# Message passing on a graph: edge tiles of 128 in place of 125, and the node update's inputs prepared another way

## The chip, the cores and the metric

The kernel runs on one core of a Trainium2 chip. The metric is the device time of one execution in microseconds (us). Engines are called PE (matmul), PEld (its weight load), DVE (vector), ACT (scalar), POOL (GpSimd, which here issues the gathers) and SP (which issues plain DMAs).

## The reference

A layer norm with a relu gives h from x (12,500 nodes, 64 features). One graph layer follows over 412,500 edges that are sorted by receiver:

```python
h = maximum(layernorm(x), 0)
m_in = concat([h[src], h[dst], edge_attr], -1)           # 64 + 64 + 32
msg  = swish(m_in @ W1 + b1) @ W2 + b2                   # 64 units
att  = softmax(swish(m_in @ Wa1 + ba1) @ Wa2 + ba2, axis=0)   # over all edges
agg  = segment_sum(msg * att, dst)
out  = x + swish(concat([h, agg], -1) @ Wu1 + bu1) @ Wu2 + bu2
```

All is float32. A node has 33 incoming edges on average, so some 1000 consecutive edges have about 30 receivers.

## The kernel before

**Node stage.** x is normalized, h is transposed into `hT` (features on partitions, kept in SBUF and written once to `hT_d`), and the product of h with the senders' part of [Wa1, W1] goes to a table in HBM, `ts_d`, of 128 columns a node; the receivers' part goes to `tr_d`.

**The group loop** (`one_pass`) does nearly all of the work. A group is K = 8 tiles of EP = 125 edges; there are NG = 413. For group g + 2, `load` issues:

- on POOL one indirect DMA per tile (L513), which gathers the senders' rows of `ts_d` into `gs`, one row per partition. A tile with odd j gathers 126 rows (WIDE), one more than it has edges;
- on SP the window of receiver rows (L534, 40 rows from the group's first receiver on) and, every fourth group, edge features and receiver numbers (L524, L527);
- on DVE the one-hot matrix of receivers (L538), and on PE the product of one-hot matrix and edge features with the window (L542), which adds the receivers' and the edges' parts in one matmul.

**Chosen groups.** In one group of three (`chosen`) the eighth tile is not gathered. ACT copies one column of `hT` per edge into `cols` (L484), at an address that it loads into a register, and PE multiplies `cols` with `stack` (L548). `numbers` loads the senders' numbers on SP, `places` works out the columns on six small DVE instructions (L467 to L473), and `burst` spreads the copies over three groups by the table `SLOTS`, some 36 to 48 per group in two portions.

**The rest of a group.** `begin(g)` adds the gathered rows (L553, DVE) and takes tanh (L556, ACT). `end(g)` makes messages and logits (L566 to L577, DVE). Every four groups `top` and `weigh` update the softmax's running maximum (L596 on PE, L603 to L610). `sum_up`, some groups later, weighs a group (`by_node`, L620 on DVE and L626 on PE), copies the sum (L632, ACT), projects it (L637, PE) and adds it into `sums` (`put`, L651 to L658, DVE). The compute instructions of the loop are pinned in program order on each engine. `gs` has seven buffers, `pe` three; POOL waits when no `gs` is free.

**Inputs of the update.** While groups 17 and later run, one of 13 node tiles is prepared every eight groups: `tile_bias` (at g % 8 of 1 and 5) reads h back from `hT_d` into `hb` on SP (L329) behind a memset of a row of ones on DVE (L327), multiplies it with Wu1's upper half and bu1 (L331) and copies the result into `bu` on ACT (L348), which goes out to `bq_d` (L351). `tile_rest` (at 3) loads x rows into another `hb` (L366), adds bu2 on DVE (L370) and writes `xb_d` (L371). `hb` has two buffers for all of these. None of these three kinds of compute instruction is pinned.

**The end.** The last groups run in smaller batches, and the update of all nodes follows. A branch to a general version (`general`) is taken only where a group's receivers do not fit its window.

Of the kernel before, what the change touches and what calls it, by code (L numbers as in the profile page):

```python
# [44 lines left out]
F32 = mybir.dt.float32  # L45
I32 = mybir.dt.int32
AF = mybir.ActivationFunctionType
ALU = mybir.AluOpType
# [3 lines left out]
DRAM = bass.MemoryType.DRAM  # L52

P = 128
EP = 125
D = 64
DE = 32
U = 64
C = 2 * U
# [13 lines left out]

EVERY = 3
PHASE = 1
SLOTS = (((0, 24), (24, 24)), ((48, 24), (72, 12)), ((84, 24), (108, 17)))
ROUND = 12582912.0
WIDE = 126
EPS = 1e-5
NEG = -3.0e38  # L80
BIG = 3.0e38


PARTS = [("pair", 4 * C), ("we", C), ("bias", C), ("wu2h", 2 * D), ("wa2", U), ("bu2", D), ("w_bu", U),
         ("w2b", U), ("wu1a", U), ("wu2", D), ("ba2", 1)]
HALVED = 4
WHY = "a receiver's number; windows past the last node are padded"

# [2 lines left out]
def gnn_kernel(ctx: ExitStack, tc: tile.TileContext, n_edges, x, src, src_row, dst, dst_row, first, edge,  # L91
# [32 lines left out]
    wu2h = part["wu2h"].rearrange("p (h d) -> p h d", h=2)  # L124
    we, bias, wa2, bu2_r, ba2_c = (part[k] for k in ("we", "bias", "wa2", "bu2", "ba2"))
    w_bu = part["w_bu"][:D + 1]
    w2b = part["w2b"][:S1]
    wu1a, wu2 = part["wu1a"][:U], part["wu2"][:U]

# [191 lines left out]
def node_bias(tc, b, v, work, ps):  # L321

    nc = tc.nc
    NB, w_bu = v["NB"], v["w_bu"]
    n = min(4, NB - b)
    hb = work.tile([D + 1, 4, P], F32, name="hb")
    nc.vector.memset(hb[D:, :, :], 1.0)  # L327
    for r in range(2):
        nc.sync.dma_start(hb[:D, r:n:2, :], v["hT_d"][r * D:(r + 1) * D, b // 2:(b + n) // 2, :])  # L329
    pb = ps.tile([P, 4, P], F32, name="mt")  # L330
    nc.tensor.matmul(pb[:U, :n, :], w_bu, hb[:, :n, :], start=True, stop=True)  # L331
    return pb[:U, :n, :]


def tile_bias(tc, c, first, v, work, ps, bus):

    nc = tc.nc
    m = min(NC, v["NB"] - c)
    if first:
        bus[c] = work.tile([U, P * NC], F32, name="bu", bufs=1)[:, :P * m]  # L340
    elif m <= 4:
        return
    i = 0 if first else 4
    n = min(4, m - i)
    pb = node_bias(tc, c + i, v, work, ps).rearrange("u b (h p) -> u h p b", h=2)
    to = bus[c].rearrange("u (h k p b) -> u k h p b", h=2, k=2, b=m // 2)
    for k in range(i // (m // 2), (i + n) // (m // 2)):
        nc.scalar.copy(to[:, k], pb[:, :, :, k * m // 2 - i:(k + 1) * m // 2 - i])  # L348
    if i + n == m:
        for h in range(2):  # L350
            nc.sync.dma_start(v["bq_d"][c // NC, h * U:(h + 1) * U, :P // 2 * m],  # L351
                              bus[c][:, h * P // 2 * m:(h + 1) * P // 2 * m])


def halves(ap, c, n, k, NB):
# [1 line left out]
    return ap.rearrange("(h p b) d -> p h b d", h=2, b=NB)[:, :, c + k * n // 2:c + (k + 1) * n // 2, :]  # L357


def tile_rest(tc, c, v, work):  # L360

    nc = tc.nc
    n = min(NC, v["NB"] - c)
    xt = work.tile([P, 4, P], F32, name="hb").rearrange("p a b -> p (a b)")[:, :n * D]
    for k in range(2):
        nc.sync.dma_start(  # L366
            xt[k * P // 2:(k + 1) * P // 2].rearrange("p (h b d) -> p h b d", h=2, d=D),
            halves(v["x"], c, n, k, v["NB"]))
    xv = xt.rearrange("p (b d) -> p b d", d=D)
    nc.vector.tensor_tensor(xv, xv, v["bu2_r"][:, None, :].to_broadcast([P, n, D]), ALU.add)  # L370
    nc.sync.dma_start(v["xb_d"][c // NC, :, :n * D], xt)  # L371


def one_pass(tc, n_edges, v):
    nc = tc.nc
    NB, T, NG, NP, NT = (v[k] for k in ("NB", "T", "NG", "NP", "NT"))
    ident, iota_w, bj, dloc, src_full, base_sb, real, unreal, far, wrong = (
        v[k] for k in ("ident", "iota_w", "bj", "dloc", "src_full", "base_sb", "real", "unreal",
                       "far", "wrong"))
    ts_d, tr_d, bq_d, xb_d, edge, dst_row = (  # L380
        v[k] for k in ("ts_d", "tr_d", "bq_d", "xb_d", "edge", "dst_row"))
# [10 lines left out]
    with ExitStack() as ctx:  # L392
# [3 lines left out]
        NH = NP // 2  # L396
        sums = keep.tile([P, NH + 2 * W], F32, name="sums")
        stand = keep.tile([P, NH + 2 * W], F32, name="stand")
        base_lo = keep.tile([1, NG + 1], I32, name="base_lo")
        base_hi = keep.tile([1, NG + 1], I32, name="base_hi")  # L400
# [35 lines left out]
        with tc.tile_pool(name="work2", bufs=2) as work2, \  # L436
# [50 lines left out]
                for i in range(EVERY):  # L487
                    columns(g + 3 + i, *SLOTS[EVERY - 1 - i][k])

            at_sp, at_lo, at_hi, bus = {}, {}, {}, {}  # L490


            tr_w = bass.AP(tensor=tr_d.tensor, offset=tr_d.offset,
# [10 lines left out]
            def load(g):  # L504

                t = g * K
                if g % NQ == 0:
                    registers(g, ENG.SP, at_sp)
                full = gather.tile([P, K, C], F32, name="gs")
                gs = gss[g] = full[:EP]  # L510
                for j in range(K - (g in chosen)):
                    rows = WIDE if j % 2 == 1 else EP
                    nc.gpsimd.indirect_dma_start(  # L513
                        out=full[:rows, j, :], out_offset=None, in_=ts_d[:, :],
                        in_offset=bass.IndirectOffsetOnAxis(ap=src_full[:rows, t + j:t + j + 1], axis=0))
                if g % NQ == 0:
                    n = min(NQ, NG - g) * E2
                    eo = eos[g // NQ % 2]
# [199 lines left out]
            for g in range(NG):  # L718
# [17 lines left out]
                burst(g, 0)  # L736
                if g + AHEAD < NG:
                    load(g + AHEAD)
                numbers(g + EVERY + 4)
                places(g + EVERY + 3)  # L740
                if more:
                    next(more)
                if g == NG - 1:
# [20 lines left out]
                if g == min(44, NG):  # L764
# [5 lines left out]
                if g == min(45, NG):  # L770
                    pin(nc.vector.tensor_reduce(worst, worst_ps, AX.X, ALU.max))
                    pin(nc.vector.tensor_scalar(wrong, worst, 0.0, None, op0=ALU.is_gt))
                if g >= 16 and g // 8 - 2 < NT:
                    c = (g // 8 - 2) * NC
                    if g % 8 in (1, 5):
                        tile_bias(tc, c, g % 8 == 1, v, work2, one_ps, bus)
                    elif g % 8 == 3:
                        tile_rest(tc, c, v, work2)

            tc.mark_branch_hint_location("again", "LikelyTaken",  # L780
                                         engines=[ENG.SP, ENG.DVE, ENG.PE, ENG.Activation])
# [271 lines left out]
def _laid_out(w):  # L1053

    import numpy as np

    first = np.concatenate([w["Wa1"], w["W1"]], axis=1)
    part = {k: np.zeros((P, n), np.float32) for k, n in PARTS}
    for r in range(2):
        for h in range(2):  # L1060
            at = (2 * r + h) * C
            part["pair"][h * D:(h + 1) * D, at:at + C] = first[r * D:(r + 1) * D]
    for r in (0, 64, 96):
        part["we"][r:r + DE] = first[2 * D:]
# [6 lines left out]
    part["w_bu"][:D + 1] = np.concatenate([w["Wu1"][:D], w["bu1"][None]])  # L1071
    part["w2b"][:S1] = np.concatenate([w["W2"], w["b2"][None]])
# [43 lines left out]
```

## Time and profile before

| | |
|---|---|
| median of 23 runs | 5638.05 us (5618.55 to 5668.15) |
| the profiled execution | 5626.18 us, its span 5624.3 us |
| mean granted clock of TensorE | 0.594 |
| first tanh of the group loop, last one | 101 us, 5573 us after the span's start |
| DMA | 398.57 MB, mean 71 GB/s |

The page counts busy time per engine, without register, semaphore and DMA-issuing instructions. A row of a group of instructions reads: line, engine, operation, output<-input, count | busy us, mean ns of one | idle us of the engine ahead of them, and what ended most of it. "issue" there is idle time in which the engine waited for nothing that the profile shows; "remote" is a semaphore whose setter it could not name. A line of the timeline begins with its start and its length in us.

### The profile page before, as it was taken

The page shows a single profiled execution, that of the slowest core. Times are in us where ns is not written, and L with a number is a line of the kernel's source. Part 1 is how long each engine was busy: PE and PEld are TensorE (multiplying, and loading weights), DVE is VectorE, ACT ScalarE, POOL GpSimd, SP SyncE. Part 2 cuts the span into 40 slices and gives each one's busy share as a digit, 9 for nine tenths or more (in the row PEclk, how much of TensorE's full clock was granted, in tenths as well). Part 3 has the DMA queues.
Part 4 walks back from the last instruction along what each step waited for, and adds up shares of the span by engine and source line. Part 5 has one row for each costly group of instructions (what it writes and reads, how often), then busy time and mean ns, then how long its engine had stood idle before and what let it go on. Part 6 is the DMA issues. An engine that isn't in the chain of part 4 may idle for free. (4 is left out here: it accounts for less than half of the span.)

```text
span 5624.3 us, 81803 instructions
## 1 busy us (share of the span) xinstructions
PE 2571.5 (46%) x11509; PEld 2005.7 (36%) x11509; DVE 3352.7 (60%) x9768; ACT 2489.0 (44%) x17651; POOL 3544.7 (63%) x3198
## 2 busy tenths in 40 slices
PE   5244444444444444444444444444444444444445
PEld 4233333333333333333333333333333333333335
DVE  6366656666556555555555565565555555555657
ACT  3244444444444444444444444444444444444422
POOL 4666666666666666666666666666666666666663
PEclk8565566666656555555555565555555555565556
DMA  7233333233232222222222222222222222222232
GB/s 228 61 73 70 74 81 78 70 80 75 68 70 65 63 63 67 58 66 61 65 66 63 63 67 59 66 61 65 66 61 65 68 58 65 61 66 65 63 81 68
DMA packets 335625, 398.57 MB, mean 71 GB/s; under 512 B 170293, under 2 KB 266088, under 8 KB 334690
## 3 DMA queue, kind: packets, MB, share of 16 engines
q0 software_dynamic: 205168, 205.98, 15.6%
q1 hardware_dynamic: 128530, 177.64, 13.2%
q10 hardware_dynamic: 1376, 9.67, 0.4%
q14 instruction: 457, 3.74, 0.2%
q8 instruction: 94, 1.54, 0.1%
HBM read 365.34 MB, written 25.72 MB: 70 GB/s over the span
## 5 line engine op out<-in xcount | busy, mean ns | idle before, releaser
L513 POOL DMA_INDIRECT gs<-ts_d,src_sb x3173 | 3527.4, 1112 | 1988.7 <-issue 1893.2
L484 ACT COPY cols<-hT 128x1 f32 x16375 | 1903.7, 188 | 2528.0 <-issue 2472.1
L542 PE MATMUL pe<-wins,eo 128*125 128x256 f32 x3304 | 1507.3, 633 | 837.1 <-DVE lg L577 250.8
L542 PEld LDWEIGHTS pe<-wins,eo 128*125 128x125 f32 x3304 | 1000.7, 319 | 1172.3 <-DVE lg L577 289.0
L637 PE MATMUL mt<-ss,w2u 65*128 65x40 f32 x826 | 226.5, 371 | 1325.9 <-DVE gm L603 583.4
L620 DVE TENSOR_SCALAR wt<-iota_w,dloc,p 125x40 f32<-125x40 f32 x3304 | 751.1, 332 | 1.6
L637 PEld LDWEIGHTS mt<-ss,w2u 65*128 65x128 f32 x826 | 209.5, 296 | 1473.1 <-issue 861.3
L626 PE MATMUL sp<-wt,acts 125*65 125x40 f32 x6608 | 721.1, 287 | 11.8 <-issue 8.4
L626 PEld LDWEIGHTS sp<-wt,acts 125*65 125x65 f32 x6608 | 684.2, 205 | 18.3 <-issue 12.0
L566 DVE SCALAR_TENSOR_TENSOR acts<-pe,gs 125x512 f32<-125x512 f32 x413 | 284.4, 689 | 572.3 <-ACT pe L556 475.7
L553 DVE TENSOR_TENSOR gs<-pe,gs 125x1024 f32<-125x1024 f32 (+1 forms) x413 | 486.4, 1178 | 177.0 <-remote 123.2
L556 ACT ACTIVATE pe<-gs 125x1024 f32<-125x1024 f32 x413 | 422.6, 1023 | 337.8 <-DMA gs<-ts_d,src_sb 128.7
L655 DVE TENSOR_TENSOR sums<-sums,mt 64x40 f32 x606 | 115.6, 191 | 489.8 <-remote 456.2
L596 PE MATMUL mt<-ident,mx 125*128 125x125 f32 x110 | 47.9, 436 | 595.1 <-remote 242.0
L538 DVE TENSOR_SCALAR eo<-dbs,bj 64x250 f32<-64x250 int32 x826 | 290.0, 378 | 17.1 <-DMA dbs<-in_dst_row_dram 7.6
L574 DVE TENSOR_TENSOR pe<-pe,w_all 125x512 f32<-125x512 f32 x413 | 288.8, 699 | 13.4
L572 DVE SCALAR_TENSOR_TENSOR pe<-pe,gs 125x512 f32<-125x512 f32 x413 | 286.8, 695 | 9.2
L577 DVE TENSOR_REDUCE lg<-pe 125x8 f32<-125x512 f32 x413 | 283.8, 687 | 9.5
L547 DVE SCALAR_TENSOR_TENSOR cols<-num,half,cols 128x125 f32<-128x125 int32 x131 | 45.6, 348 | 372.1 <-ACT cols L484 320.2
L596 PEld LDWEIGHTS mt<-ident,mx 125*128 125x128 f32 x110 | 20.0, 181 | 606.7 <-remote 440.9
L691 DVE SCALAR_TENSOR_TENSOR total<-total,scale,psum 125x1 f32<-125x1 f32 x110 | 23.5, 214 | 294.0 <-ACT p L610 270.6
L548 PE MATMUL pe<-stack,cols 128*125 128x128 f32 x262 | 79.9, 400 | 203.5 <-DVE cols L547 125.5
(125 smaller groups left out, 1211.7 us busy)
## 6 DMA issues: line engine op xcount, KB each, us to landing
eo<-in_edge_dram SPq DMA_DIRECT2D x103, 500.0 KB
dbs<-in_dst_row_dram SPq DMA_DIRECT2D x206, 250.0 KB
gs<-ts_d,src_sb POOLq DMA_INDIRECT x3173
wins<-tr_d SPq DMA_DIRECT2D x826, 32.0 KB
num<-in_src_row_dram SPq DMA_DIRECT2D x131, 62.5 KB
ts_d<-ts SPq DMA_DIRECT2D x5, 896.0 KB
tr_d<-tr ACTq DMA_DIRECT2D x5, 896.0 KB
hT_d<-hT ACTq DMA_DIRECT2D x1, 3136.0 KB
```

The source lines that it names most:

```text
L484: pin(nc.scalar.copy(to[:, first + i:first + i + 1], hT[:, bass.ds(regs[i], 1)]))
L513: nc.gpsimd.indirect_dma_start(out=full[:rows, j, :], out_offset=None, in_=ts_d[:, :], in_offset=bass.IndirectOffsetOnAxis(ap=src_full[:ro ...
L538: pin(nc.vector.tensor_scalar(eo[:WR, e], db[:, e], bj[g // NQ % 2 * WR:(g // NQ % 2 + 1) * WR, g, h:h + 1], None, op0=ALU.is_equal))
L542: pin(nc.tensor.matmul(pe[:, 2 * q:2 * q + 2, :], eo[:, q * EP:(q + 1) * EP], win[:, q // 2, :, :], start=True, stop=q < H - 1 or g not in ...
L553: pin(nc.vector.tensor_tensor(gss[g][:, :n, :], pes[g][:, :n, :], gss[g][:, :n, :], ALU.add))
L556: pin(nc.scalar.activation(pes[g], gss[g], AF.Tanh))
L566: pin(nc.vector.scalar_tensor_tensor(acts[g % ACTS][:, :, 0:U], th[:, :, U:C], 1.0, gs[:, :, U:C], op0=ALU.add, op1=ALU.mult))
L572: pin(nc.vector.scalar_tensor_tensor(att, th[:, :, 0:U], 1.0, gs[:, :, 0:U], op0=ALU.add, op1=ALU.mult))
L574: pin(nc.vector.tensor_tensor(att, att, wa2[:EP, None, :].to_broadcast([EP, K, U]), ALU.mult))
L620: pin(nc.vector.tensor_scalar(wt[:, j, :], iota_w[:EP, j // H, :], dloc[:, g * K + j:g * K + j + 1], p[:, k + j:k + j + 1], op0=ALU.is_equ ...
L626: pin(nc.tensor.matmul(sp, acts[g % ACTS][:, j, :], wt[:, j, :], start=j == 0, stop=j == K - 1))
L637: pin(nc.tensor.matmul(pp, w2u.rearrange("s h u -> s (h u)"), sps.pop(g), start=True, stop=True))
```

## The change

EP becomes 128, so a group has 1024 edges, NG is 403 and a tile fills all partitions. Every gather takes EP = 128 rows, and WIDE goes. The last portion of columns grows from 17 to 20, so that a chosen tile has 128 of them.

`tile_bias` no longer reads `hT_d`: one matmul of a block-diagonal weight (`w_bup`, Wu1's upper half twice) with `hT` as it lies in SBUF gives four node blocks at once, and two DVE additions of `bu1` write them to `bu`. All of it is pinned and stands right behind `places` in the loop. The DMAs to `bq_d` are issued at g % 8 of 7 (`tile_bias_out`). `tile_rest` is split over three groups: x rows are asked for at 0 into a buffer of their own (`xt`), bu2 is added at 3, `xb_d` is written at 6. The numbers of `numbers` and `places` are written out with the same values. Two small tables of bases share a tile, and the check of the windows moves from groups 44 and 45 to 46 and 47.

```diff
-EP = 125
+EP = 128
-SLOTS = (((0, 24), (24, 24)), ((48, 24), (72, 12)), ((84, 24), (108, 17)))
+SLOTS = (((0, 24), (24, 24)), ((48, 24), (72, 12)), ((84, 24), (108, 20)))
-WIDE = 126
...
 def tile_bias(tc, c, first, v, work, ps, bus):
...
-    pb = node_bias(tc, c + i, v, work, ps).rearrange("u b (h p) -> u h p b", h=2)
+    pb = ps.tile([P, 4, P], F32, name="mt")[:, :n // 2, :]
+    pin(nc.tensor.matmul(pb, v["w_bup"], v["hT"][:, (c + i) // 2:(c + i + n) // 2, :], start=True, stop=True))
     to = bus[c].rearrange("u (h k p b) -> u k h p b", h=2, k=2, b=m // 2)
-    for k in range(i // (m // 2), (i + n) // (m // 2)):
-        nc.scalar.copy(to[:, k], pb[:, :, :, k * m // 2 - i:(k + 1) * m // 2 - i])
-    if i + n == m:
-        for h in range(2):
-            nc.sync.dma_start(v["bq_d"][c // NC, h * U:(h + 1) * U, :P // 2 * m],
-                              bus[c][:, h * P // 2 * m:(h + 1) * P // 2 * m])
+    for b in range(i, i + n):
+        r, k = b % 2, b // (m // 2)
+        if b >= i + 2 and m // 2 > 1:
+            continue
...
+        pin(nc.vector.tensor_scalar(
+            to[:, k, :, :, at:at + 2 * q - 1:2],
+            pb[rows, (b - i) // 2:(b - i) // 2 + q, :].rearrange("u q (h p) -> u h p q", h=2),
+            v["bu1"][rows], None, op0=ALU.add))
...
-def tile_rest(tc, c, v, work):
+def tile_rest(tc, c, step, v, work, rest):
...
+    if step == 0:
+        xt = rest[c] = work.tile([P, 4 * P], F32, name="xt", bufs=1)[:, :n * D]
+        for k in range(2):
+            nc.sync.dma_start(
+                xt[k * P // 2:(k + 1) * P // 2].rearrange("p (h b d) -> p h b d", h=2, d=D),
+                halves(v["x"], c, n, k, v["NB"]))
+    elif step == 1:
+        xv = rest[c].rearrange("p (b d) -> p b d", d=D)
+        tc.keep_in_program_order(
+            nc.vector.tensor_tensor(xv, xv, v["bu2_r"][:, None, :].to_broadcast([P, n, D]), ALU.add))
+    else:
+        nc.sync.dma_start(v["xb_d"][c // NC, :, :n * D], rest.pop(c))
...
-                full = gather.tile([P, K, C], F32, name="gs")
-                gs = gss[g] = full[:EP]
+                gs = gss[g] = gather.tile([P, K, C], F32, name="gs")[:EP]
                 for j in range(K - (g in chosen)):
-                    rows = WIDE if j % 2 == 1 else EP
                     nc.gpsimd.indirect_dma_start(
-                        out=full[:rows, j, :], out_offset=None, in_=ts_d[:, :],
-                        in_offset=bass.IndirectOffsetOnAxis(ap=src_full[:rows, t + j:t + j + 1], axis=0))
+                        out=gs[:, j, :], out_offset=None, in_=ts_d[:, :],
+                        in_offset=bass.IndirectOffsetOnAxis(ap=src_sb[:, t + j:t + j + 1], axis=0))
...
-                numbers(g + EVERY + 4)
-                places(g + EVERY + 3)
+                numbers(g + 7)
+                places(g + 6)
+                if g >= 16 and g // 8 - 2 < NT and g % 8 in (1, 5):
+                    tile_bias(tc, (g // 8 - 2) * NC, g % 8 == 1, v, work2, one_ps, bus)
                 if more:
                     next(more)
...
-                    if g % 8 in (1, 5):
-                        tile_bias(tc, c, g % 8 == 1, v, work2, one_ps, bus)
-                    elif g % 8 == 3:
-                        tile_rest(tc, c, v, work2)
+                    if g % 8 == 7:
+                        tile_bias_out(tc, c, v, bus)
+                    elif g % 8 in (0, 3, 6):
+                        tile_rest(tc, c, g % 8 // 3, v, work2, rest)
```

More of the change, by code (lines that the diff above doesn't have):

```diff
@@ L84 @@
 PARTS = [("pair", 4 * C), ("we", C), ("bias", C), ("wu2h", 2 * D), ("wa2", U), ("bu2", D), ("w_bu", U),
-         ("w2b", U), ("wu1a", U), ("wu2", D), ("ba2", 1)]
+         ("w2b", U), ("wu1a", U), ("wu2", D), ("ba2", 1), ("w_bup", 2 * U), ("bu1", 1)]
 HALVED = 4
@@ L126, in gnn_kernel @@
     w_bu = part["w_bu"][:D + 1]
+    w_bup, bu1 = part["w_bup"], part["bu1"]
     w2b = part["w2b"][:S1]
@@ L337, in tile_bias @@
     nc = tc.nc
+    pin = tc.keep_in_program_order
     m = min(NC, v["NB"] - c)
@@ L344, in tile_bias @@
     n = min(4, m - i)
-    pb = node_bias(tc, c + i, v, work, ps).rearrange("u b (h p) -> u h p b", h=2)
+    pb = ps.tile([P, 4, P], F32, name="mt")[:, :n // 2, :]
+    pin(nc.tensor.matmul(pb, v["w_bup"], v["hT"][:, (c + i) // 2:(c + i + n) // 2, :], start=True, stop=True))
     to = bus[c].rearrange("u (h k p b) -> u k h p b", h=2, k=2, b=m // 2)
-    for k in range(i // (m // 2), (i + n) // (m // 2)):
-        nc.scalar.copy(to[:, k], pb[:, :, :, k * m // 2 - i:(k + 1) * m // 2 - i])
-    if i + n == m:
-        for h in range(2):
-            nc.sync.dma_start(v["bq_d"][c // NC, h * U:(h + 1) * U, :P // 2 * m],
-                              bus[c][:, h * P // 2 * m:(h + 1) * P // 2 * m])
+    for b in range(i, i + n):
+        r, k = b % 2, b // (m // 2)
+        if b >= i + 2 and m // 2 > 1:
+            continue
+        q = 2 if m // 2 > 1 else 1
+        rows = slice(r * U, (r + 1) * U)
+        at = b - k * (m // 2)
+        pin(nc.vector.tensor_scalar(
+            to[:, k, :, :, at:at + 2 * q - 1:2],
+            pb[rows, (b - i) // 2:(b - i) // 2 + q, :].rearrange("u q (h p) -> u h p q", h=2),
+            v["bu1"][rows], None, op0=ALU.add))
@@ L355, in halves, with tile_bias_out @@
+def tile_bias_out(tc, c, v, bus):
+    m = min(NC, v["NB"] - c)
+    for h in range(2):
+        tc.nc.sync.dma_start(v["bq_d"][c // NC, h * U:(h + 1) * U, :P // 2 * m],
+                             bus[c][:, h * P // 2 * m:(h + 1) * P // 2 * m])
 def halves(ap, c, n, k, NB):
     return ap.rearrange("(h p b) d -> p h b d", h=2, b=NB)[:, :, c + k * n // 2:c + (k + 1) * n // 2, :]
-def tile_rest(tc, c, v, work):
+def tile_rest(tc, c, step, v, work, rest):
     nc = tc.nc
     n = min(NC, v["NB"] - c)
[L364 to L371, printed above, removed]
+    if step == 0:
[10 more added lines that the diff above has]
+        nc.sync.dma_start(v["xb_d"][c // NC, :, :n * D], rest.pop(c))
@@ L376, in one_pass @@
     NB, T, NG, NP, NT = (v[k] for k in ("NB", "T", "NG", "NP", "NT"))
-    ident, iota_w, bj, dloc, src_full, base_sb, real, unreal, far, wrong = (
-        v[k] for k in ("ident", "iota_w", "bj", "dloc", "src_full", "base_sb", "real", "unreal",
+    ident, iota_w, bj, dloc, src_sb, base_sb, real, unreal, far, wrong = (
+        v[k] for k in ("ident", "iota_w", "bj", "dloc", "src_sb", "base_sb", "real", "unreal",
                        "far", "wrong"))
@@ L398, in one_pass @@
         stand = keep.tile([P, NH + 2 * W], F32, name="stand")
-        base_lo = keep.tile([1, NG + 1], I32, name="base_lo")
-        base_hi = keep.tile([1, NG + 1], I32, name="base_hi")
+        bases = keep.tile([33, NG + 1], I32, name="bases")
+        base_lo, base_hi = bases[0:1], bases[32:33]
         nc.vector.memset(base_lo, 0)
@@ L488, in burst @@
                     columns(g + 3 + i, *SLOTS[EVERY - 1 - i][k])
-            at_sp, at_lo, at_hi, bus = {}, {}, {}, {}
+            at_sp, at_lo, at_hi, bus, rest = {}, {}, {}, {}, {}
             tr_w = bass.AP(tensor=tr_d.tensor, offset=tr_d.offset,
@@ L763, in one_pass @@
                     pin(nc.vector.tensor_reduce(far[:, 1:2], dloc, AX.X, ALU.min, negate=True))
-                if g == min(44, NG):
+                if g == min(46, NG):
                     worst = small.tile([EP, 1], F32, name="worst", bufs=1)
@@ L769, in one_pass @@
                     pin(nc.tensor.transpose(worst_ps, worst.to_broadcast([EP, EP]), ident[:EP, :EP]))
-                if g == min(45, NG):
+                if g == min(47, NG):
                     pin(nc.vector.tensor_reduce(worst, worst_ps, AX.X, ALU.max))
@@ L1071, in _laid_out @@
     part["w_bu"][:D + 1] = np.concatenate([w["Wu1"][:D], w["bu1"][None]])
+    for r in range(2):
+        part["w_bup"][r * D:(r + 1) * D, r * U:(r + 1) * U] = w["Wu1"][:D]
+    part["bu1"][:, 0] = np.tile(w["bu1"], 2)
     part["w2b"][:S1] = np.concatenate([w["W2"], w["b2"][None]])
```

## Prediction

> **What bounds the kernel now.** I read the page first: no engine is busy for more than 63% of the span, so no engine's plain work is the bound, and the question is what the engines wait for. The chain of work that ended last holds only the last memsets and says nothing. The groups of the page name two long streams of small instructions, and the answer lies in how they share time:
>
> ```profile
> span 5624.3 us, 81803 instructions
> PE 2571.5 (46%) x11509; PEld 2005.7 (36%) x11509; DVE 3352.7 (60%) x9768; ACT 2489.0 (44%) x17651; POOL 3544.7 (63%) x3198
> L513 POOL DMA_INDIRECT gs<-ts_d,src_sb x3173 | 3527.4, 1112 | 1988.7 <-issue 1893.2
> L484 ACT COPY cols<-hT 128x1 f32 x16375 | 1903.7, 188 | 2528.0 <-issue 2472.1
> ```
>
> POOL issues 3173 gathers of 1.112 us; ACT copies 16375 single columns, and sits idle 2472.1 us between them for a reason that the profile does not show ("issue"). ACT's own waits in front of the tanh (L556) are 337.8 us in all, so ACT is the engine that is never ahead. Why its copies are slow shows in its timeline:
>
> ```profile
> 3009.91 2.32 ACT L484 COPY cols<-hT 128x1 f32 x24 [0.60 <-issue]
> 3014.51 1.77 ACT L484 COPY cols<-hT 128x1 f32 x18 [0.18 <-issue]
> ...
> 3026.37 0.28 ACT L484 COPY cols<-hT 128x1 f32 x2 [0.44 <-issue]
> 3027.11 0.28 ACT L484 COPY cols<-hT 128x1 f32 x2 [0.46 <-issue]
> 3027.85 0.19 ACT L484 COPY cols<-hT 128x1 f32 x1 [0.46 <-issue]
> ```
>
> There are two paces: 24 copies in 2.32 us, one per 0.09 us, and one or two copies per 0.73 us. In the slow pace the register move ahead of a copy (the trace has it, the page does not count it) takes about 0.7 us in place of 37 ns; 1868 of them do, 1309 us together. The timeline of POOL shows what goes with it:
>
> ```profile
> 1999.31 1.21 POOL L513 DMA_INDIRECT gs<-ts_d,src_sb  x1 [0.30 <-issue]
> 2000.82 1.00 POOL L513 DMA_INDIRECT gs<-ts_d,src_sb  x1 [0.30 <-issue]
> 2002.12 1.21 POOL L513 DMA_INDIRECT gs<-ts_d,src_sb  x1 [0.30 <-issue]
> 2003.64 1.00 POOL L513 DMA_INDIRECT gs<-ts_d,src_sb  x1 [0.30 <-issue]
> ...
> 2019.51 1.21 POOL L513 DMA_INDIRECT gs<-ts_d,src_sb  x1 [9.23 <-issue]
> ```
>
> Gathers of 125 rows (even j) take 1.21 us and those of 126 rows (odd j) 1.00 us, 0.30 us apart, until POOL pauses for a free `gs` buffer (9.23 us here). ACT turns fast within about a microsecond of such a pause and slow again some 6 us after POOL resumes, as if its instructions pass only while POOL is not working at a gather, with a store that a pause refills. The table of windows puts a number on that:
>
> ```profile
> core 0: us, PE busy (x) PEld busy (x) DVE busy (x) ACT busy (x) POOL busy (x), PEclk, DMA share, GB/s
> 340.00:970.00 630.00, 307.69 (x1359) 233.81 (x1358) 394.28 (x1154) 295.06 (x2166) 415.11 (x374) 0.61 0.32 76
> 2000.00:2630.00 630.00, 281.37 (x1248) 219.37 (x1248) 367.71 (x1086) 288.75 (x2105) 397.17 (x358) 0.58 0.28 64
> 2630.00:3260.00 630.00, 286.39 (x1267) 222.77 (x1265) 366.73 (x1078) 282.41 (x2043) 403.60 (x364) 0.58 0.27 63
> 3890.00:4520.00 630.00, 285.97 (x1278) 224.18 (x1276) 369.03 (x1089) 289.33 (x2113) 401.09 (x362) 0.57 0.28 64
> ```
>
> Time in which POOL was not busy, per ACT instruction: (630-397.17)/2105 = 0.111 us, then 0.111 and 0.108. It is constant. A fit over the 1237 slow moves between 1800 and 5400 us, elapsed time against POOL's busy time and ACT's instructions (register moves counted apart), gives 1.00 us per us of POOL and 0.052 us per ACT instruction, with a spread of 1.4 us; by ACT's count alone the spread is 3.4 us. So time = POOL's busy time + 0.110 us x ACT's shown instructions. Over the program: 3527.4 + 17651 x 0.110 = 5469 us, and first to last tanh are 5472 us apart. The window at 340 gives 0.099: the law is good to some 4%.
>
> **The groups.** A group becomes 8 x 128 edges, so 412,500 edges are 403 groups in place of 413. Per-group work of PE, DVE and SP falls 2.4%, off the path. With 128 partitions the elements per partition are the same (1024 for L553 and L556), so one instruction costs the same; only L538 (250 to 256), L547, L596 and the six small ones of `places` grow 2.4%, and the edge rows grow by as much as the groups fall. Columns go from 131 x 125 = 16375 to 127 x 128 = 16256.
>
> **The gathers.** 403 x 8 - 127 = 3097 in place of 3173, all of 128 rows. No row shows such a gather. Upper end: the 125-row one scaled by rows, 1.213 x 128/125 = 1.24 us. Lower end: by the trace's packets a 125-row gather comes with 60 small ones of 4 and 32 bytes and a 126-row one with 20; on the line through 1.213 and 1.000 us, the 16 of 4 bytes that are always there give 0.98. I take 1.00, the row of 126, the nearest in size. POOL: 3097 x 1.00 = 3097, 430.4 us less than 3527.4, all of it on the path.
>
> The packets of before are 4096 and 512 bytes: 1652 x 15 + 1521 x 14 = 46074 and 1652 x 5 + 1521 x 14 = 29554, just the counts in the trace, so 25 rows lie on each of 5 engines or 9 on each of 14. The Trainium skill (DMA: Bandwidth & Descriptors, section "Why a DMA increments its semaphore by 16 and not by 1") says that the engine count is the largest up to 16 that divides the rows, which would be 16 engines of 8 rows here; no run shows that yet. By the line of rows per engine (25 at 1.213 us, 9 at 1.000) an estimate from that page's count is 0.986 us, and the sum would be 43 us lower.
>
> **ACT.** 119 copies, 10 tanh, 10 `ss` copies, 3 x 3 of `weigh` and the 26 bias copies (L348) go: 174 x 0.110 = 19.1 us on the path.
>
> **The bias and the x rows.** The waits that go:
>
> ```profile
> DVE hb L370 <- DMA hb<-in_x_dram: 53.1, 8, 15.4
> DVE hb L327 <- remote: 30.0, 3, 10.8
> DVE hb L327 <- DMA gs<-ts_d,src_sb: 21.7, 2, 10.8
> ```
>
> In all, DVE idles 90.1 us before L327 and 61.9 before L370. I cost that at nothing: in the stretch that holds this work (groups 17 to 112) a group took 13.04 us, later 13.4, so these stalls did not show. What moves: 25 memsets of 0.485 us and 50 loads of `hT_d` on SP's queue go; the matmul (0.938 us) becomes one of 128x256, near L305's 0.382; the 26 copies become 50 adds on DVE, by L538's 0.378 us 19 us against 12.1 for the memsets. The new wait: DVE's adds wait for the bias matmul, which stands on PE behind L542 and, in a chosen group, behind L548, which itself waits for DVE's L547. That is 0.4 + 0.4 us and a handover, some 1.3 us, 25 times, 33 us; behind it wait `by_node` and `end`. DVE is 60% busy and ACT has copies queued, so I take nothing and keep 33 us for the range (150 the other way, if the old stalls were on the path). On SP, x loads go out in step 0, `xb_d` in step 6, `bq_d` in step 7, each ahead of only later window loads. `numbers` and `places` keep their distances (7 and 6); the two base tables in one tile, the check at 46 and 47 and 129 more weight columns cost under 1 us.
>
> The Trainium skill (SBUF — State Buffer, the note on the trap "DVE blocks DMA") speaks against more work on DVE: an operation in a two-port mode locks POOL out while it writes descriptors. The trace disagrees in size: the 1521 gathers of 126 rows lie between 0.992 and 1.002 us from 5% to 95%, beside DVE at 60%.
>
> **The sum.** 5626.2 (the profiled execution) - 430.4 - 19.1 = 5176.7; that execution lies 11.9 us under the median of 23, so 5189 us, called 5190.
>
> **The rivals.** (B) ACT's pace is its own and POOL only follows. Then the time goes with ACT's instructions: 10441 in five windows of 630 us from 2000 on is 3.31 per us, 174 fewer are 53 us, 5585 us. For it: ACT's average rate is steady. Against it: the slow pace ends when POOL pauses, and the fit. (C) The stalls come with the gathers' small packets, 60 or 20 falling to 16, and vanish. Then POOL is next: 3097 x 1.30 = 4026 (0.30 us between gathers), half of the 1031 us of its long pauses, head and tail 160: 4700 us. Against it: packet counts fit no better than busy time. (D) The slower side: a gather of 128 rows costs POOL as much per row as one of 125. Then 3097 x 1.24 = 3840, 313 more, less 19: 5930 us. It decides from (3527.4 + 19.1)/3097 = 1.145 us on. For it: between 125 and 126 rows something other than size sets the price, and only two points are known; against it: 126 is nearer.
>
> **How the numbers follow.** The sum (A) 0.55: by 0.98 us a gather it gives 5125; with a law that is 4% off (3097 x 0.04 = 124 us either way) and the new wait's 33 us, it reaches from 5000 to 5350. B 0.22, C 0.08, D 0.15. The range, 4950 to 5640, holds A, B and the near side of C and leaves out D and the rest of C, under 2 in 10. A measurement of this kernel tells 0.2% from no change, about 11 us; B's upper edge gives the 0.03 within that. Faster 0.82, slower 0.15.
>
> **What would show it.** L513 at x3097 and 1.00 us; POOL near 3100 busy in a span near 5175; windows in which (time - POOL busy)/ACT instructions is again 0.11; ACT's idle before L484 well under 2472. L327 gone and no long wait at the new DVE adds. If L513 is at 1.00 and the span near 5570, POOL never held ACT; if L513 is above 1.15, the gather's price was wrong; if the idle before L484 all but vanishes, C was right.

## The result, and the profile after

The changed kernel took 6027.01 us in the median of 8 runs (6019.42 to 6033.37), the kernel before 5638.47 us in 62 runs: a ratio of 1.0683 [1.0664, 1.0703]. It became slower, where 5190 us was forecast. The profiled execution's span is 6010.1 us, 385.8 us more than before.

The kernel before does not itself take one time: in the first measurement it took 5638 us, in three of the later ones (in each, a few kernels ran one after another on one chip) 5380, 5605 and 5418 us, called **held** below, and in four others 4598, 4598, 4598 and 4608 us, called **free**. Chip 8 gave 5380 us in one measurement and 4608 us in another. A kernel is compared only with the kernel before of its own measurement.

The page of the changed kernel, its span, its engines, and the two streams of the prediction:

```profile
span 6010.1 us, 80416 instructions
PE 2565.8 (43%) x11238; PEld 1993.3 (33%) x11238; DVE 3276.1 (55%) x9553; ACT 2405.9 (40%) x17477; POOL 2959.9 (49%) x3122
L530 POOL DMA_INDIRECT gs<-ts_d,src_sb x3097 | 2942.7, 950 | 2960.5 <-issue 2889.2
L503 ACT COPY cols<-hT 128x1 f32 x16256 | 1848.2, 187 | 3072.4 <-issue 3022.6
```

The counts are those of the prediction (3097 gathers, 16256 copies, 174 fewer instructions on ACT), and a gather became cheaper than forecast, 0.950 us. POOL's busy time fell by 584.8 us, yet its idle time in front of gathers rose from 1988.7 to 2960.5 us, and ACT's in front of copies from 2528.0 to 3072.4. POOL's timeline shows what that idle time is made of:

```profile
1994.49 0.95 POOL L530 DMA_INDIRECT gs<-ts_d,src_sb  x1 [0.30 <-issue]
1995.74 0.95 POOL L530 DMA_INDIRECT gs<-ts_d,src_sb  x1 [0.31 <-issue]
2005.64 0.94 POOL L530 DMA_INDIRECT gs<-ts_d,src_sb  x1 [8.95 <-issue]
2006.89 0.95 POOL L530 DMA_INDIRECT gs<-ts_d,src_sb  x1 [0.30 <-issue]
```

There are gathers 1.25 us apart, and then a pause in which no `gs` buffer is free. Adding up all of the trace's gathers, the even gaps of 0.305 us between them, what gaps of over 0.8 us have beyond that (the pauses), and head and tail, gives the whole span of either kernel to within 4 us:

| us | gathers | even gaps | pauses | head and tail | sum |
|---|---|---|---|---|---|
| before | 3173 x 1.112 | 968 | 969 (188 of them) | 158 | 5623 |
| after | 3097 x 0.950 | 944 | 1966 (255 of them) | 154 | 6006 |

So the gathers and gaps give back 608 us, and the pauses take 997 us more. POOL pauses because those that empty `gs` are late, and ACT is: the same slow pace as before, but slower. This is its timeline:

```profile
3022.30 0.19 ACT L503 COPY cols<-hT 128x1 f32 x1 [1.24 <-issue]
3023.76 0.19 ACT L503 COPY cols<-hT 128x1 f32 x1 [1.26 <-issue]
3025.16 0.19 ACT L503 COPY cols<-hT 128x1 f32 x1 [1.21 <-issue]
3026.61 0.19 ACT L503 COPY cols<-hT 128x1 f32 x1 [1.25 <-issue]
```

It is one copy per 1.44 us, where the kernel before passed one or two per 0.73 us. The windows put the prediction's own number on it:

```profile
core 0: us, PE busy (x) PEld busy (x) DVE busy (x) ACT busy (x) POOL busy (x), PEclk, DMA share, GB/s
340.00:970.00 630.00, 270.22 (x1173) 209.34 (x1172) 352.22 (x1011) 263.30 (x1968) 311.20 (x327) 0.57 0.26 65
2000.00:2630.00 630.00, 263.27 (x1158) 202.23 (x1158) 337.53 (x1002) 263.00 (x1969) 313.45 (x330) 0.56 0.24 60
3890.00:4520.00 630.00, 270.25 (x1185) 208.66 (x1185) 345.64 (x1022) 263.81 (x1980) 319.72 (x337) 0.58 0.25 60
```

(630-313.45)/1969 = 0.161 us of POOL not being busy per ACT instruction, and 0.162 and 0.157 in the others. Before it was 0.111: the constant of the law is none.

The new wait that the prediction kept 33 us for is there, and it is longer:

```profile
DVE bu L356 <- remote: 115.0, 15, 10.7
```

A group takes 14.5 to 14.7 us from the sixteenth on, with this work and without it, so these 115 us are not what made the kernel slower.

### The profile page after: what moved, and what is told of

It is laid out like the page before. It is cut to its first block, busy times and chain, and to the rows that moved or that the text cites. A ratio compares the mean times of both kernels' runs of the same rounds, so it can differ in the third digit from the quotient of the medians.

```text
span 6010.1 us, 80416 instructions
## 1 busy us (share of the span) xinstructions
PE 2565.8 (43%) x11238; PEld 1993.3 (33%) x11238; DVE 3276.1 (55%) x9553; ACT 2405.9 (40%) x17477; POOL 2959.9 (49%) x3122
## 5 line engine op out<-in xcount | busy, mean ns | idle before, releaser
L530 POOL DMA_INDIRECT gs<-ts_d,src_sb x3097 | 2942.7, 950 | 2960.5 <-issue 2889.2
L503 ACT COPY cols<-hT 128x1 f32 x16256 | 1848.2, 187 | 3072.4 <-issue 3022.6
L559 PE MATMUL pe<-wins,eo 128*128 128x256 f32 x3224 | 1490.2, 638 | 852.7 <-DVE eo L555 431.5
L559 PEld LDWEIGHTS pe<-wins,eo 128*128 128x128 f32 x3224 | 985.7, 323 | 1164.0 <-DVE eo L555 469.0
L637 DVE TENSOR_SCALAR wt<-iota_w,dloc,p 128x40 f32<-128x40 f32 x3224 | 723.3, 311 | 29.5 <-issue 27.7
L643 PE MATMUL sp<-wt,acts 128*65 128x40 f32 x6448 | 718.2, 292 | 10.2 <-issue 6.8
L643 PEld LDWEIGHTS sp<-wt,acts 128*65 128x65 f32 x6448 | 685.4, 212 | 11.7 <-issue 7.6
L570 DVE TENSOR_TENSOR gs<-pe,gs 128x1024 f32<-128x1024 f32 (+1 forms) x403 | 474.7, 1178 | 66.7 <-issue 49.8
L573 ACT ACTIVATE pe<-gs 128x1024 f32<-128x1024 f32 x403 | 412.1, 1023 | 244.6 <-DMA gs<-ts_d,src_sb 80.5
L591 DVE TENSOR_TENSOR pe<-pe,w_all 128x512 f32<-128x512 f32 x403 | 281.8, 699 | 16.2 <-issue 2.2
L589 DVE SCALAR_TENSOR_TENSOR pe<-pe,gs 128x512 f32<-128x512 f32 x403 | 280.4, 696 | 15.1 <-remote 3.2
```

What stands on the lines that cost most here:

```text
L503: pin(nc.scalar.copy(to[:, first + i:first + i + 1], hT[:, bass.ds(regs[i], 1)]))
L530: nc.gpsimd.indirect_dma_start(out=gs[:, j, :], out_offset=None, in_=ts_d[:, :], in_offset=bass.IndirectOffsetOnAxis(ap=src_sb[:, t + j:t ...
L559: pin(nc.tensor.matmul(pe[:, 2 * q:2 * q + 2, :], eo[:, q * EP:(q + 1) * EP], win[:, q // 2, :, :], start=True, stop=q < H - 1 or g not in ...
L570: pin(nc.vector.tensor_tensor(gss[g][:, :n, :], pes[g][:, :n, :], gss[g][:, :n, :], ALU.add))
L573: pin(nc.scalar.activation(pes[g], gss[g], AF.Tanh))
L589: pin(nc.vector.scalar_tensor_tensor(att, th[:, :, 0:U], 1.0, gs[:, :, 0:U], op0=ALU.add, op1=ALU.mult))
```

## The experiments

In all of them the sum of the table above is used: gathers times their distance (their own length and the gap of 0.305 us), plus pauses, plus head and tail.

### The parts by themselves

The rows of the gathers alone, in the kernel before (gathers take 128 rows; the tiles stay at 125 edges):

```diff
-                    rows = WIDE if j % 2 == 1 else EP
+                    rows = 128
```

> The kernel of before with one edit: every gather takes 128 rows (the rows past the tile's 125 edges are gathered into partitions that nobody reads). Theory S (a gather of 128 rows holds ACT back more than the mix of 125 and 126 rows): POOL's gathers take 0.95 us as in the changed kernel, yet ACT's idle before the column copies grows from 2472 us to about 3000, and the time is 5950 to 6150 us. Theory M (the moved bias and x-row work holds the loop) and theory G (the group of 1024 edges does): no slower than 5640, and by the law of the prediction (POOL busy + 0.11 us x ACT instructions) near 5130.

Measured, in a free measurement: 4087.20 us against 4598.27, ratio 0.8888 [0.8873, 0.8903]. Its page:

```profile
span 4084.9 us, 81803 instructions
L513 POOL DMA_INDIRECT gs<-ts_d,src_sb x3173 | 3004.8, 947 | 1016.1 <-issue 880.3
L484 ACT COPY cols<-hT 128x1 f32 x16375 | 1617.9, 187 | 747.8 <-issue 731.5
```

Without a single pause, 3173 x 1.252 + 112 = 4085 us. ACT's idle time in front of the copies, 2472.1 us for "issue" in the kernel before, is 731.5 us here, and no register move takes 0.7 us.

The other part alone: the changed kernel with EP = 125 and gathers of 125 and 126 rows, so that what differs from before is the bias and the x rows.

```diff
-EP = 128
+EP = 125
-SLOTS = (((0, 24), (24, 24)), ((48, 24), (72, 12)), ((84, 24), (108, 20)))
+SLOTS = (((0, 24), (24, 24)), ((48, 24), (72, 12)), ((84, 24), (108, 17)))
+WIDE = 126
...
+                    rows = WIDE if j % 2 == 1 else EP
```

> The changed kernel with tiles of 125 edges and gathers of 125 and 126 rows as before, so that only the bias and x-row part of the change is left. Theory S and G: 5590 to 5660 us, as before. Theory M: 5950 us or more.

Measured: 4596.99 us, ratio 0.9997 [0.9987, 1.0006]. This part is worth nothing in a free measurement. In a held one it was not run alone. The kernel differs from the one before by this part only, so its profile also stands in for that of the kernel before in a free measurement. The first lines of its page:

```profile
span 4598.7 us, 81829 instructions
PE 2414.4 (53%) x11509; PEld 1939.7 (42%) x11509; DVE 3388.6 (74%) x9793; ACT 2202.6 (48%) x17625; POOL 3538.8 (77%) x3198
```

POOL is as busy as in the profile of before (3538.8 against 3544.7 us), but the span is 1026 us shorter, and 3173 x 1.415 + 107 = 4597: the pauses are gone, and no register move is slow. What the prediction took for a property of the kernel was there only in held measurements.

### ACT's copies

The changed kernel with `chosen` empty (every tile is gathered: 3224 gathers, no column copies), and with the copies from fixed columns in place of registers:

```diff
-            chosen = {g for g in range(8, NG - 12) if g % EVERY == PHASE}
+            chosen = set()
```

> The changed kernel with no chosen group: all eight tiles of every group are gathered, ACT copies no column. Theory S (what makes the time is ACT's small instructions, held back while POOL gathers): ACT falls to some 1300 instructions, POOL becomes the bound at 403 x 8 x 1.25 us = 4030 us plus 150 us of head and 150 of tail, 4300 to 4600 us. If it is the gathers' landing or the DMA engines that make the time: 3224 gathers in place of 3097, 6000 us or more.

```diff
-                _, regs = nc.values_load_multi_w_load_instructions(
-                    at[0:1, first:first + n], engines=[ENG.Activation], min_val=0, max_val=NP // 2 - 1,
-                    skip_runtime_bounds_check_because=WHY)
...
-                    pin(nc.scalar.copy(to[:, first + i:first + i + 1], hT[:, bass.ds(regs[i], 1)]))
+                    pin(nc.scalar.copy(to[:, first + i:first + i + 1], hT[:, 7 * i:7 * i + 1]))
```

> The changed kernel with the same 16256 column copies, but from fixed columns of hT: no register is loaded and no register move stands ahead of a copy (so the columns are not the senders' ones). If only register moves are held back: every copy goes at 0.09 us, the idle before the copies all but vanishes, 4300 to 4800 us. If every ACT instruction is held back alike, the copies alone are half as many instructions: the slow pace stays in the timeline, some 5200 us.

Measured, in the same free measurement: 4136.49 us, ratio 0.8997 [0.8982, 0.9012], and 3983.34 us (one run; its columns are not the senders'). Both are POOL's stream: 3224 x 1.250 + 106 = 4136, and 3097 x 1.251 + 106 = 3980. Since no move is slow in this measurement, they do not tell what the moves do in a held one.

### The same in another measurement, and the gathers' length

The changed kernel again, and the kernel before with 125, 126 and 127 rows in every gather (the edit of `rows` as above):

> The changed kernel, unchanged, beside the kernel before on the same chip. Theory P (the slow register moves of ACT belong to the chip or its state, not to the kernel; without them POOL's stream of gathers sets the time): where the kernel before takes about 4600 us, this takes 3097 x (0.947 + 0.305) = 3877 us plus about 115 us of head and tail, 3990 to 4030 us, a ratio of 0.87. Theory K (the first measurement's ratio belongs to the kernel pair): a ratio near 1.07 whatever the kernel before takes. Where the kernel before takes about 5640 us, both say 1.07.

> The kernel of before with gathers of 125 rows for every tile. Without slow register moves: 3173 x (1.213 + 0.305) + 115 = 4930 us. With them (the kernel before near 5640 us) and theory S (ACT is held back by how wide a gather is spread): fewer engines per gather, so faster than before in spite of longer gathers, 5300 to 5600 us.

> The kernel of before with gathers of 126 rows for every tile. Without slow register moves: 3173 x (0.998 + 0.305) + 115 = 4250 us. With them and theory S: slower than before, 5800 to 6100 us.

> The kernel of before with gathers of 127 rows for every tile, a prime number. If POOL's price goes with the rows that the longest-loaded engine gets (25 on 5 engines 1.213 us, 9 on 14 engines 0.998, 8 on 16 engines 0.947) and 127 rows fall to one engine: 0.85 + 0.0145 x 127 = 2.7 us a gather and about 9600 us. If it goes with odd and even: 1.2 us and about 4900 us. With slow register moves and theory S (one engine): ACT at its fast pace throughout.

This measurement was a held one; the kernel before took 5380.37 us. The changed kernel took 5926.84 us, ratio 1.1001 [1.0937, 1.1066]: slower again. Of the others there is one run each: 4931.86, 5895.53 and 9177.42 us. The pages of 125, 126 and 127 rows, in this order:

```profile
span 4930.0 us, 81803 instructions
L513 POOL DMA_INDIRECT gs<-ts_d,src_sb x3173 | 3851.0, 1214 | 1020.8 <-issue 914.7
L484 ACT COPY cols<-hT 128x1 f32 x16375 | 1635.6, 187 | 820.4 <-issue 802.7
```

```profile
span 5893.7 us, 81803 instructions
L513 POOL DMA_INDIRECT gs<-ts_d,src_sb x3173 | 3165.1, 998 | 2624.0 <-issue 2488.3
L484 ACT COPY cols<-hT 128x1 f32 x16375 | 1895.4, 188 | 2923.5 <-issue 2894.7
```

```profile
L513 POOL DMA_INDIRECT gs<-ts_d,src_sb x3173 | 8097.5, 2552 | 1018.0 <-issue 909.3
```

This turns the law over, and the 5300 to 5600 us expected of 125 rows were missed too. With the longer gather of 125 rows in every place, POOL is busy for 324 us more than in the kernel before, and the kernel is 449 us faster than the kernel before of its measurement; with the shorter one of 126 it is 515 us slower. At 1.214 us a gather (1.519 us from one to the next) the pauses come to 4 us, 3173 x 1.519 + 107 + 4 = 4931; at 0.998 us (1.302 apart) they come to 1606 us. In long rows of gathers without a pause, behind the first dozen, ACT passes (register moves and semaphore waits counted) about 8.0 instructions per us at the distance of 1.52 us, 1.8 at 1.30, and 1.3 in the changed kernel at 1.25. The kernel before, where the two lengths alternate (1.417 on average), passes 3.2. With the first dozen counted in, the order is the same: 7.6, 5.5, 4.5 and 4.0 from the widest distance to the closest. So what holds ACT is not how long POOL works at gathers; it goes with how often they come, or with how many DMA engines each uses (5, 14 or 16, see the last section), which changes along with that here. At 125 rows 83 register moves still take 0.7 us, where free traces have none.

At 127 rows one gather takes 2.552 us, and no move is slow.

### Fewer rows, and gathers set apart

The changed kernel without columns once more, and the kernel before with gathers of 25 and of 112 rows (the `gs` buffers become seven fixed ones that are cleared first):

> The changed kernel with no chosen group, as in e3, to have it where ACT's register moves are slow too. Theory S (time = gathers x a price that grows with the engines a gather is spread on + 0.054 us per ACT instruction, or POOL's own pace if that is longer; price 1.23 us for 128 rows, fitted to e5): 3224 x 1.23 + 4000 x 0.054 + 155 = 4340 us at most, and POOL's pace gives 4140. If the gathers themselves run short there: 5000 us or more.

```diff
-                full = gather.tile([P, K, C], F32, name="gs")
+                full = next_gs()
...
-                    rows = WIDE if j % 2 == 1 else EP
+                    rows = 25
```

> The kernel of before with gathers of 25 rows (100 rows of each tile are not gathered), which by the packets of the 125-row gather would lie on 5 engines, in POOL's shortest time, about 0.9 us. Where register moves are slow: theory S1 (the number of engines holds ACT): few slow moves, POOL's pace, 3173 x 1.2 + 120 = 3950 us. Theory S2 (how often gathers come, whatever their spread): as slow as gathers of 128 rows, 5800 to 6100 us. Theory S3 (rows or bytes): faster than before, no slow moves. Where there are no slow moves: 3900 to 4000 us.

> The kernel of before with gathers of 112 rows (13 rows of each tile are not gathered): 16 engines of 7 rows. Where register moves are slow: theory S1 (engines): as with 128 rows, 5800 to 6100 us. Theory S3 (rows): clearly faster than with 126 rows, below 5600. Where there are none: 3173 x (0.93 + 0.305) + 115 = 4030 us.

And the changed kernel with the gathers set apart by a memset of POOL behind each (both pinned in program order):

```diff
-                    nc.gpsimd.indirect_dma_start(
+                    pin(nc.gpsimd.indirect_dma_start(
...
+                    pin(nc.gpsimd.memset(filler, 0.0))
```

> The changed kernel with a POOL memset of 192 columns after each gather, which stretches the distance of two gathers from 1.25 us to about 1.55, that of 125-row gathers in e6. Where register moves are slow: theory S2 (frequency): ACT is held back no more, 3097 x 1.55 + 115 = 4920 us. Theory S1 (engines): a gather still costs 1.23 us of the time that ACT shares, 1.55 - 1.23 leaves 0.32 us or 6 ACT instructions a gather where 11.8 are needed, so 5700 to 6000 us. Where there are none: 4920 us.

The measurement was free (4597.56 us before). The changed kernel without columns took 4137.18 us, ratio 0.8996 [0.8981, 0.9011]; 25 and 112 rows took 4076.87 and 4051.65 us, and the memsets 4486.28 us (one run each; the memset made the distance 1.40 us and not 1.55). No move was slow in any of them, so the question (does the hold go with the number of DMA engines that a gather uses, or with how often gathers come?) had no answer here. The two with fewer rows show that a gather of 25 or of 112 rows costs POOL about as much as one of 128: 0.945 and 0.937 us beside 0.947.

The changed kernel and the one with memsets once more:

> The changed kernel, unchanged, once more. Theory P (without slow register moves POOL's stream sets the time): beside a kernel before of about 4600 us it takes 3097 x (0.946 + 0.305) = 3874 plus 115, 3990 to 4030 us, ratio 0.87. Theory K: ratio near 1.07 there too. Beside a kernel before of 5400 to 5640 us: 5900 to 6050 us, as in e5.

> The changed kernel with a POOL memset after each gather, as in e12, whose gathers come every 1.41 us and which took 4486 us where no register move was slow. Where they are slow: theory S2 (frequency) puts it between the mix (1.41 us apart on average, 5380 to 5640 us) and 125 rows (1.52 us apart, 4930 us), so 5300 us or less; theory S1 (engines): 1.41 us apart, of which a gather of 16 engines takes 1.23, so 3097 x 1.23 + 36500 x 0.054 + 155 = 5930 us, as without the memsets.

That measurement was held (5605.32 us before). The changed kernel: 6000.45 us, 1.0703 [1.0685, 1.0722]. With the memsets: 5617.87 us (one run), that is 383 us faster, though POOL has 865 us more to do:

```profile
span 5616.1 us, 83514 instructions
L531 POOL DMA_INDIRECT gs<-ts_d,src_sb x3097 | 2975.0, 961 | 1649.7 <-issue 1591.9
L534 POOL MEMSET filler<- 128x192 f32 x3097 | 864.6, 279 | 26.3 <-DMA tr_d<-tr 21.5
```

The gathers come 1.399 us apart, the pauses shrink from 1948 to 1109 us, and ACT passes about 3.1 instructions per us in long rows of gathers, beside 1.3 without the memsets and 3.2 in the kernel before. The changed kernel with and without memsets gathers 128 rows over 16 engines, so here it is the distance alone that counts. The time is not the 5300 us or less that this reading was expected to give, though: at 1.399 us the kernel takes as long as the kernel before, whose distance is nearly the same but whose gathers use other numbers of DMA engines. Work of POOL as such does not hold ACT: the memsets are work too.

The changed kernel and the 25 rows in a further measurement, and the 25 rows in one more:

> The changed kernel, unchanged. Beside a kernel before of about 4600 us (no slow register moves): 3990 to 4030 us, ratio 0.87, by POOL's stream; theory K says 1.07. Beside one of 5400 us or more: 5900 to 6050 us.

> The kernel of before with gathers of 25 rows as in e10: 5 engines, 1.25 us apart. Where register moves are slow: theory S2 (how often gathers come) 5800 to 6050 us, as with 128 rows at the same distance; theory S1 (how many engines they are spread on) POOL's pace, 4080 us as in e10; theory S3 (bytes moved, a fifth of the usual) also near 4080. Where no move is slow: 4077 us again.

> The kernel of before with gathers of 25 rows, as in e10 and e16. Where register moves are slow (the kernel before at 5400 us or more): theory S2 (frequency) 5800 to 6050 us; theories S1 (engines) and S3 (bytes) near 4080 us. Where none is slow: 4076 us.

Both were free (4598.16 and 4608.17 us before). The changed kernel took 3987.13 us, ratio 0.8671 [0.8657, 0.8686], the same kernel that is 1.07 to 1.10 in held ones. Its page:

```profile
span 3985.0 us, 80416 instructions
L530 POOL DMA_INDIRECT gs<-ts_d,src_sb x3097 | 2932.6, 947 | 993.3 <-issue 850.7
L503 ACT COPY cols<-hT 128x1 f32 x16256 | 1605.0, 187 | 717.1 <-issue 714.2
```

3097 x 1.252 + 107 = 3984 us: POOL's stream without a pause. The 25 rows took 4075.75 and 4086.55 us; this kernel never met a held measurement, so a spread over few DMA engines was never seen there.

### Is it ACT's copies that are held, or ACT?

By now my theory was that the slow register moves in front of the copies make the time. The test is the changed kernel without columns in a held measurement:

> The changed kernel with no chosen group, as in e3 and e9. Where register moves are slow (the kernel before at 5400 us or more): if the time there is made by ACT's small instructions under the gathers, POOL's pace decides, 4140 us, at most 4340 (3224 x 1.23 + 4000 x 0.054 + 155); if the gathers themselves run short there, 5000 us or more. Where no move is slow: 4137 us.

The measurement was held (5417.73 us before). Measured: 5580.29 us, ratio 1.0301 [1.0272, 1.0330], where the theory gave 4140. The theory fell. ACT has 1221 shown instructions in this kernel, and no register moves, and still 159 pauses of POOL take 1389 us: 3224 x 1.254 + 1389 + 153 = 5585. The span and a group of its page, and a line each of the waits of ACT and of SP's queue:

```profile
span 5584.9 us, 45445 instructions
L649 ACT COPY ss<-sp 65x40 f32<-65x40 f32 x403 | 75.4, 187 | 2783.3 <-remote 2568.7
```

```profile
ACT ss L649 <- remote: 2568.7, 169, 23.6
SPq L551 <- remote: 2480.9, 124, 27.0
```

The same ACT wait of the same kernel in a free measurement (e9):

```profile
ACT ss L649 <- PE sp L643: 12.7, 7, 2.7
```

The work that is waited for is not late. This is one such wait in its timeline from 2996 to 3032 us (PE, ACT, SP's queue and POOL):

```profile
2996.85 1.48 PE L643 MATMUL sp<-wt,acts 128*65 128x40 f32 x16
...
2999.26 1.03 ACT L573 ACTIVATE pe<-gs 128x1024 f32<-128x1024 f32 x1 [5.64 <-DVE gs L570]
...
3003.52 0.00 SPq L544 DMA_DIRECT2D dbs<-in_dst_row_dram  x1
...
3005.50 3.78 PE L559 MATMUL pe<-wins,eo 128*128 128x256 f32 x8 [7.17 <-issue]
...
3017.26 0.95 POOL L530 DMA_INDIRECT gs<-ts_d,src_sb  x1 [0.30 <-issue]
3018.51 0.94 POOL L530 DMA_INDIRECT gs<-ts_d,src_sb  x1 [0.30 <-issue]
3023.42 0.19 ACT L649 COPY ss<-sp 65x40 f32<-65x40 f32 x1 [23.13 <-remote]
3023.45 8.39 SPq L551 DMA_DIRECT2D wins<-tr_d  x4
...
3031.28 0.94 POOL L530 DMA_INDIRECT gs<-ts_d,src_sb  x1 [11.83 <-issue]
```

The copy L649 needs the matmuls L643, which ended at 2998.33, and ACT itself was done with the tanh at 3000.29. It starts 23.13 us later, at the same time as SP's next load of a window; in between SP's small instructions took 0.7 us each until 3007.7 and then none ran at all. PE and DVE ran on meanwhile (their matmuls L559 and the work of `end` stand at 3005 to 3010) until they needed ACT. POOL's last gather ended at 3019.45, and ACT and SP moved 4.0 us after it. In this trace 147 of the 403 copies L649 begin more than 3 us after ACT and PE had done what comes before them, 2627 us together; in the free one none does.

What is late is the signal. L649 waits for a semaphore that PE's instructions raise, and the trace records when a semaphore is updated. In the wait shown, five updates stand between 3023.17 and 3023.34, some 42 ns apart, though no instruction of PE that raises it ended between 3009.28 and 3024.31; ACT moves within 0.1 us of the fifth. Of this semaphore's recorded updates 1062 of 3071 lie more than 1 us behind the end of any such instruction, in the free trace 2 of 3443, and 143 of the 152 waits of over 3 us ahead of L649 end right behind such a late update.

So it is no matter of copies alone. In a held measurement PE's updates arrive late while gathers come in a close row, and ACT and SP, which need them, stand, until POOL runs out of free `gs` buffers; POOL's pause lets them through, and the row begins anew. The lateness goes with the distance: nine tenths of the updates come within 1.4 us at 1.519 us from gather to gather, 5.4 at 1.417, 5.6 at 1.399, 7.6 at 1.302 and 7.6 in the changed kernel. The slow register moves come on top, for they wait for no semaphore; whether late updates and slow moves have one cause is not shown. In the changed kernel the pace around a pause shows the hold too: ACT (without register moves) passes 0.7 to 1.2 instructions per us in the last 6 us of a row, 5 to 8 per us from 3 us after the last gather on, and again 1 to 2 from 6 us after POOL has resumed.

Two simpler causes do not fit. The gathers' transfers are no slower: their packets take 119 ns on average in the held trace without columns and 121 in the free one. Nor is it the granted clock of TensorE, which is 0.573 in the changed kernel's held profile and 0.638 in its free one: a matmul of L559, the largest group, takes 638 ns and 630. A third was not tested. The changed kernel's trace has 28472 records of semaphore updates in the first measurement and 82199 in the free one, for the same instructions, so in the held one most are missing; and every timed run comes with a span and a clock, so none is known to be without recording. Whether the recording has a part in the hold is open.

## Why the prediction was wrong

**The step that failed is the law,** "time = POOL's busy time + 0.110 us x ACT's shown instructions", with the reading behind it, "as if its instructions pass only while POOL is not working at a gather". Its term for the gathers, 430.4 us less, "all of it on the path", came out as 608 us less of gathers and gaps and 997 us more of pauses. Over the whole program (span less POOL busy)/ACT instructions is 0.118 us before, 0.154 with 126 rows, 0.175 after, and 0.060 with 125 rows. In the kernel before, two lengths of gather alternated in a fixed mix, so POOL's busy time and the number of gathers rose together, and a fit inside one kernel could not tell a price per microsecond from a price per gather. The change moved the two apart: 584.8 us less busy, nearly as many gathers, closer together. A fixed price per gather is not it either, for the memsets take 383 us off with as many gathers. The runs show a hold that grows as gathers come closer:

| gathers apart, us | rows | ACT instructions per us, behind the first dozen of a row | pauses, us | span, us |
|---|---|---|---|---|
| 1.519 | 125 | 8.0 | 4 | 4930 |
| 1.417 | 125 and 126 in turn (before) | 3.2 | 969 | 5624 |
| 1.399 | 128 and a memset | 3.1 | 1109 | 5616 |
| 1.302 | 126 | 1.8 | 1606 | 5894 |
| 1.255 | 128 (after) | 1.3 | 1966 | 6010 |

(From three held measurements, so rows differ by a few per cent for that too.)

**What was right.** The counts of gathers, groups and copies. That the bias and the x rows cost nothing (0.9997), in a free measurement. Their new wait was mis-sized, though: 33 us were kept, and L356 waits 90.7 us for its matmul in the changed kernel's free trace and 115.0 us for "remote" in the held one, where 15 of its 25 waits end on a late update of PE; by the time of a group it was off the path. The 128-row gather's place near the 126-row one: 0.950 us, where 1.00 was taken, a little under the lower bound of 0.98. The packets after are 49552 of 4096 bytes and 49552 of 4, 16 of each for each of 3097 gathers, so 8 rows lie on each of 16 engines, as the Trainium skill (DMA: Bandwidth & Descriptors, "Why a DMA increments its semaphore by 16 and not by 1") has it; the estimate from that count, 0.986 us, was nearer than 1.00.

**The rivals.** B (ACT's pace is its own) is refuted: the pace changes with the gathers' distance. C (the stalls vanish with the small packets and POOL is next) has the outcome of free measurements, at 3987 us instead of 4700, since no pause is left at all; but its cause is not there: the kernel before is without stalls in them too, and in held ones the small packets fell to 16 and the pauses grew. D (a gather dearer than 1.145 us) is refuted at 0.950 us, although the time came out past its 5930. The slower side came from a mechanism that I had no rival for: that a shorter gather can cost more because it lets the next one come sooner. The evidence was within reach as a question: the slow moves end when POOL pauses, and that fits a hold per gather as well as a hold per busy microsecond.

**What stays open.** Why one measurement is held and another free is not known; the profiles cover one core and cannot show other work on the chip. How gathers make PE's updates late and register moves slow is not seen either, and the recording of the trace is not ruled out. Whether the number of DMA engines that a gather uses has a part in it stays open beside the distance: the kernel with 25 rows met three free measurements and no held one, and only the pair at 1.399 and 1.417 us speaks against it. The parts of the change were not run alone in a held measurement; the nearest is the kernel before with 126 rows everywhere. No kernel was the best in both sorts. In held ones it is the one with 125 rows everywhere (4931.86 us against 5380.37, one run), whose 3173 x 1.519 us would by this sum be its time in free ones too, which was not run; in free ones, of those that leave nothing out, the changed one (0.867). Tiles of 128 with an even distance of 1.5 us were not tried.

## What to carry to other kernels

A constant found by a fit inside one trace holds for the mix in that trace; before a change moves it, ask whether a price per microsecond, a price per piece and a price that depends on how closely the pieces come can be told apart there, and if not, keep all of them for the range with both signs. In an "issue" or "remote" wait whose work has long been done, on two engines at once, the data are not late: look at when the signal came, and at what a third engine does at the moment at which both move again. And where a stream of transfers both sets the pace and slows those who consume them, the shortest transfer need not be the best one: run a longer, evenly spaced one beside it, in the same measurement.

## What the runs showed of the hardware

- In the lengths tried, a gather's price on POOL goes with its rows on the fullest DMA engine, and levels off below 9 (rows per engine worked out from the packets' sizes at 512 bytes a row): 127 rows (15 packets of 4096 bytes and one of 3584, beside 225 of 32 bytes; by these counts all rows lie on one engine) took 2.552 us, 125 rows (25 on each of 5) 1.214, 126 (9 on each of 14) 0.998, 128 (8 on each of 16) 0.947, 112 (7 on each of 16) 0.937, 25 (5 on each of 5) 0.945.
- In held measurements gathers 1.25 us apart left ACT about one instruction per us, and an instruction of ACT whose work ahead was done stood for up to 23.6 us (SP's longest wait is 27.0 us); at 1.52 us apart there was next to no hold (4 us of pauses). In the changed kernel 2090 small ACT instructions (register moves and semaphore waits) and 372 of SP took 0.6 to 0.8 us, and not one of the 4201 on DVE and PE.
- In held traces updates of PE's semaphore came late: 977 of 3165 by more than 1 us in the changed kernel, beside 2 of 3445 in its free trace.
- The kernel before, unchanged, took between 4598 and 5638 us from one measurement to another, and the sign of what this change did went with it: 0.867 in a free one, 1.068, 1.070 and 1.100 in held ones.
